# Moving two batches of a decoder's last feed-forward block into the attention loop of later batches, in 32 pieces

## The chip, the core and the metric

One core of one Trainium2 chip runs the whole program. The metric is the device time of one execution in microseconds (us), lower is better. A core has five engines that run their own queues in order: TensorE (PE, with its weight loads PEld), VectorE (DVE), ScalarE (ACT), GpSimd (POOL) and the DMA queue of SyncE (SP).

## What is computed

Two decoder layers over x of 4 batches x 512 rows x 256 columns, all float32. The part that matters here is layer 1, after its self-attention: cross-attention of 16 heads against 1601 context rows, a residual and a layer norm, and then a feed-forward block whose weights are dequantized from int32:

```python
scores = jnp.einsum('bhqd,bhkd->bhqk', Q, K) * SCALE        # layer 1 cross-attention
...
h = (x - mu) * jax.lax.rsqrt(var + EPS) * ln_gamma + ln_beta  # the last block
y = jax.nn.silu(h.reshape(-1, H) @ w1 + fc1_bias)             # 256 -> 1024
z = y @ w2 + fc2_bias                                         # 1024 -> 256
return residual + 0.5 * z.reshape(residual.shape)
...
x = _layernorm(x + _L1_ffn_ref(x, ...))
```

In that last line the block's residual is x itself, so the sum is 2x + 0.5 z. Batches are independent of one another through all of layer 1.

## The kernel before

Layer 1 is one instruction order written out by hand (a manual schedule: each engine runs its instructions as the Python code emits them). Its attention is a loop over `units` (line 1208): for self-attention and then for cross-attention, for each batch b, four groups g of four heads. A cross-attention unit has 13 steps k over the context rows (12 of 128 rows and one of 65), each of two halves of two heads. A half emits, in this order (lines 1848 to 1860): a score matmul (`scores`, line 1467), the two matmuls of a "slot" of the next unit that serve its row maxima (`slot1`, line 1419, recorded as line 202 with tiles one<-kc,qt), the second score matmul, two exponentials on ScalarE (`exponents`, line 1481), two maximum reductions on VectorE (`reduce`, line 1424), and half of the weighted sum of the step before (`weighted`, line 1494, tile po). Scores contract over 32 rows, so the two scores and the two slot matmuls of a half sit in four different row groups of the array and run together; the trace counts every float32 matmul as two records.

Other work is put between these steps by three lists for each unit. `starts` runs ahead of a unit. `extras` are spread evenly over its steps, at the end of a step; in a step that takes one (`filled`, line 1839) the whole weighted sum goes into the first half as one matmul of 512 columns instead of two of 256. `quiet` gives up one item after each half, and what is left at the unit's end runs at once. The last unit has no slots left; it emits all four scores of a step together.

Score tiles come from a pool of three PSUM banks (`spare`, tag s2), slots and most extras from one of four (`one`).

Cross-attention of batch b ends in `finish` (line 1504): copy of po, transposes, division (`divided`), two transposes (`turned`), four projections (`projected`) and a layer norm (`normalize_apart`), all as extras and quiet items of the next batch's first unit. Two units later `block_input(b)` (line 1622) norms again, transposes into xT[b] and makes 2x plus a bias on GpSimd (`twice`). The block's weights f1 and f2 are loaded and multiplied out by eight `dequantized` items in the quiet list of the unit (3, 2), that is batch 3, group 2 (line 1815). They use the tiles raw and swp, which the rotary step `rotated` (line 1294) also uses.

The block itself, `block(b)` (line 1650), runs for all four batches after the last unit. A `first(f)` makes 128 of the 1024 hidden columns for 512 rows: two matmuls of 512 columns into one bank and one Silu on ScalarE. A `second(t)` makes 128 output rows: eight matmuls of 256 columns, and a VectorE instruction that adds to x. After each second row tile come the final layer norm (on VectorE, with the reciprocal root by Newton steps, `rstd_newton`) and the store. The end of batch 3's own cross-attention, its two norms and its `block_input`, the generator `ending`, is dealt out one item after each piece of the block:

```python
firsts, seconds = zip(*(block(b) for b in range(B)))
rest = ending()
for work in (firsts[0], firsts[1], seconds[0], firsts[2], seconds[1], firsts[3], seconds[2], seconds[3]):
    if work is firsts[3]:
        for _ in rest:
            pass
    for f in work:
        f()
        next(rest, None)
```

Of the kernel before, what the change touches and what calls it, by code (L numbers as in the profile page):

```python
# [9 lines left out]
F32 = mybir.dt.float32  # L10
# [29 lines left out]
def decoder(ctx: ExitStack, tc: tile.TileContext, a: dict, out: bass.AP):  # L40
# [587 lines left out]
    with tc.tile_pool(name="p2", bufs=2) as p2, ExitStack() as ordered:  # L628
# [538 lines left out]
    with ExitStack() as s4:  # L1167
# [137 lines left out]
        def flush(n):  # L1305
            while len(going) > n:
                going.pop(0)()
# [342 lines left out]
        def block(b):  # L1650
# [46 lines left out]

            return [lambda f=f: first(f) for f in range(NF)], [lambda t=t: second(t) for t in range(NT)]


        order1 = [(u, s) for u in units for s in range(slots1(u))]
        ends1, n = {}, 0
# [109 lines left out]
        work = [loads[0], loads[1], nothing, nothing]  # L1812
        for i in range(8):
            work += [products[i], loads[i + 2] if i < 6 else nothing, nothing]
        quiet[index[3, 2, True]] += work

        for i, u in enumerate(units):
            for f in starts[i]:
                f()
            nk = NKT if u[2] else NT  # L1820
            work = extras[i]
            ran = 0
            alone.append(u)
            while done["n"] < ends1[u] + LEAD:
                reduces = [next1() for _ in range(min(2, ends1[u] + LEAD - done["n"]))]
                for f in reduces:
                    f()
                if ran < len(work) - nk // 2:
                    work[ran]()
                    ran += 1  # L1830
            alone.clear()
            del work[:ran]
            ran = 0
            for k in range(nk):
                behind = (u, k - 1)
                if k == 0:
                    behind = (units[i - 1], (NKT if units[i - 1][2] else NT) - 1) if i else None

                filled = ran < len(work) and ran * nk < (k + 1) * len(work)
                if u == units[-1]:  # L1840
                    pairs = [[scores(u, k, half, h) for h in range(2)] for half in range(2)]
                    for half in range(2):
                        next1()
                        exponents(u, k, half, pairs[half])
                        if quiet[i]:
                            quiet[i].pop(0)()
                    weighted(*behind)
                for half in range(2 if u != units[-1] else 0):
                    first = scores(u, k, half, 0)
                    reduce = next1()  # L1850
                    exponents(u, k, half, (first, scores(u, k, half, 1)))
                    reduce()
                    if quiet[i]:
                        quiet[i].pop(0)()
                    if behind is None:
                        pass
                    elif not filled:
                        weighted(*behind, half * 256, half * 256 + 256)
                    elif half == 0:
                        weighted(*behind)  # L1860
                while filled and ran < len(work) and ran * nk < (k + 1) * len(work):
                    work[ran]()
                    ran += 1
            while ran < len(work):
                work[ran]()
                ran += 1
            while quiet[i]:
                quiet[i].pop(0)()
        weighted(units[-1], NKT - 1)

        def ending():
# [19 lines left out]

    late_a.close()
    late_w.close()
# [139 lines left out]
```

## Time and profile before

| what | us |
|---|---|
| runs | 2378.8, 2392.78, 2396.34; median 2392.78 |
| the profiled execution | 2391.23, its span 2389.1 |
| cross-attention, 16 units | 1456 to 2265.2 |
| of which units (2,1) to (3,3) | 1934.0 to 2265.3 |
| last block and its end | 2265.2 to 2389.1 |
| mean granted clock of TensorE over the span | 0.971 |

How to read it. A timeline line gives the start in us from the span's start, the time from the start of the first to the end of the last of the records that it merges, the engine, the line of the kernel, the operation, what is written and read, the shapes, how many records, and in brackets how long the engine had been idle and what ended that. A windows line gives, for a stretch of time, its length and then the busy time (and the count) of PE, PEld, DVE, ACT and POOL, the granted TensorE clock, and the DMA share and rate. A line "a/b/c" of one source line gives the shortest, median and longest duration in ns.

### The profile page before, as it was taken

To read this page: it belongs to the slowest core of one execution; us is meant where nothing else is said; L and a number is where in the kernel's file an instruction comes from. 1 tells how busy PE (TensorE), PEld (TensorE's weight loads), DVE (VectorE), ACT (ScalarE), POOL (GpSimd) and SP (SyncE) were. 2 spreads that over 40 slices of the span, in tenths; PEclk is the share of its full clock that TensorE was granted. 3 is DMA by queue.
4 is the path that set the end of the run, shared out by engine and by line. 5 is a ranking of instruction groups with operands and counts; after the bars stand their busy time and mean duration, and the time that the engine had idled before them with its cause. 6 is when DMAs were issued, how large, how long until landed. Compare 5 with 4: busy or idle time off the path is not lost.

```text
span 2389.1 us, 36156 instructions
## 1 busy us (share of the span) xinstructions
PE 2270.9 (95%) x14448; PEld 1287.5 (54%) x14448; DVE 1231.9 (52%) x2918; ACT 1063.0 (44%) x2103; POOL 369.3 (15%) x383
## 2 busy tenths in 40 slices
PE   7899999977999999879999999999999999999998
PEld 4768577756888988633333334333333333333366
DVE  1433334431333434455656667666766776777234
ACT  1111222223554645424555443655656565666730
POOL 1010001130222122335230010211112010000000
PEclk9999999988999999989999998999999999999999
DMA  8400311135887767352221310112110010100000
GB/s 302 177 0 1 133 55 46 46 126 190 333 307 269 291 260 297 108 173 85 67 87 54 116 37 1 38 33 72 63 39 28 25 60 15 64 1 21 29 9 27
DMA packets 77099, 244.13 MB, mean 102 GB/s; under 512 B 11640, under 2 KB 34686, under 8 KB 64638
## 3 DMA queue, kind: packets, MB, share of 16 engines
q1 hardware_dynamic: 60126, 141.96, 17.2%
q0 software_dynamic: 13632, 89.32, 9.9%
q10 hardware_dynamic: 3168, 10.48, 1.2%
q8 instruction: 116, 1.90, 0.3%
q14 instruction: 57, 0.47, 0.1%
HBM read 196.12 MB, written 56.77 MB: 106 GB/s over the span
## 4 chain that ended last, share of the span: by engine, by line
PE 53%; ACT 1%; DVE 1%; DMA 1%; POOL 1%; issue 0%; SPq 0%; DVEq 0%; ACTq 0%; POOLq 0%
PE s L1467 23%; PE one L202 12%; PE po L1494 12%; PE s L202 3%; PE s L1477 1%; PE one L1452 1%; PE one L1515 1%; DMA cx<-in_ctxT 1%; ACT x L171 1%; DVE one L1426 0%; ACT ex L1481 0%; DMA y<-ys,yrows 0%; DVE pm L1424 0%; PE one L1536 0%; DMA qd<-q 0%
## 5 line engine op out<-in xcount | busy, mean ns | idle before, releaser
L1481 ACT ACTIVATE ex<-s 128x512 f32<-128x512 f32 (+1 forms) x1062 | 578.0, 594 | 465.5 <-PE s L1467 225.3
L1424 DVE TENSOR_REDUCE pm<-one 128x1 f32<-128x512 f32 x768 | 492.8, 685 | 161.1 <-PE s L1467 106.1
L1467 PE MATMUL s<-q,kc 32*128 32x512 f32 x1612 | 528.8, 639 | 0.8 <-ACT ex L1481 0.8
L202 PE MATMUL one<-kc,qt 32*128 32x512 f32 (+1 forms) x2048 | 483.5, 563 | 0.3 <-DVE pm L1424 0.3
L1467 PEld LDWEIGHTS s<-q,kc 32*128 32x128 f32 x1612 | 166.1, 179 | 203.1 <-issue 170.0
L1494 PE MATMUL po<-ex,v 128*32 128x256 f32 (+3 forms) x2688 | 251.5, 443 | 0.3 <-ACT ot L1507 0.3
L1426 DVE CUSTOM_DVE_ANT_0 one<-one,c_diagq 128x512 f32<-128x512 f32 x256 | 171.9, 715 | 97.8 <-PE one L202 88.2
L1494 PEld LDWEIGHTS po<-ex,v 128*32 128x32 f32 (+1 forms) x2688 | 54.1, 108 | 253.1 <-issue 246.4
L1467 PE MATMUL s<-q,ks 32*128 32x512 f32 x512 | 180.6, 658 | 6.2 <-ACT ex L1481 4.9
L202 PEld LDWEIGHTS one<-kc,qt 32*128 32x128 f32 x2048 | 164.5, 188 | 11.8 <-DVE pm L1424 7.4
L202 PE MATMUL bank<-eWo,g 128*128 128x256 f32 x608 | 140.3, 387 | 11.5 <-DVE rb L997 8.2
L202 PE MATMUL one<-ks,qt 32*128 32x512 f32 x512 | 149.6, 664 | 0.0
L202 PE MATMUL wide<-xbT,eWi 128*128 128x128 f32 (+1 forms) x960 | 141.0, 308 | 4.0 <-DVE xbT L943 4.0
L977 DVE TENSOR_TENSOR g<-g,sg 128x1024 f32<-128x1024 f32 x38 | 46.4, 1224 | 180.3 <-ACT sg L975 171.9
L202 PEld LDWEIGHTS wide<-xbT,eWi 128*128 128x128 f32 x960 | 131.1, 194 | 13.4 <-issue 4.2
L202 PE MATMUL wide<-xbT,eWg 128*128 128x128 f32 (+1 forms) x960 | 137.0, 303 | 0.0
L202 PEld LDWEIGHTS bank<-eWo,g 128*128 128x128 f32 x608 | 115.5, 194 | 31.0 <-DVE rb L997 12.2
L1299 POOL TENSOR_TENSOR raw<-raw,c_cos 128x512 f32<-128x512 f32 (+1 forms) x32 | 35.0, 1093 | 626.5 <-DVE swp L1298 626.5
L202 PEld LDWEIGHTS wide<-xbT,eWg 128*128 128x128 f32 x960 | 128.1, 191 | 6.6
L1467 PEld LDWEIGHTS s<-q,ks 32*128 32x128 f32 x512 | 53.4, 187 | 83.9 <-issue 64.6
L975 ACT ACTIVATE g<-wide,eWi 128x128 f32<-128x128 f32 (+1 forms) x240 | 72.6, 410 | 56.8 <-PE wide L202 56.4
L202 PE MATMUL wide<-ctxT,q 128*128 128x512 f32 (+1 forms) x256 | 91.3, 510 | 0.8 <-DVE q L669 0.8
(346 smaller groups left out, 2948.5 us busy)
## 6 DMA issues: line engine op xcount, KB each, us to landing
xs<-zero SPq DMA_DIRECT2D x32, 512.0 KB
kc<-kcd SPq DMA_DIRECT2D x16, 800.5 KB
eWo<-in_eWo SPq DMA_DIRECT2D x8, 1408.0 KB
eWi<-in_eWi SPq DMA_DIRECT2D x8, 1028.0 KB
eWg<-in_eWg SPq DMA_DIRECT2D x8, 1028.0 KB
qt<-qd SPq DMA_DIRECT2D x32, 256.0 KB
ctxT<-in_ctxT SPq DMA_DIRECT2D x4, 1601.0 KB
cx<-in_ctxT SPq DMA_DIRECT2D x12, 512.0 KB
```

The costliest lines, as they stand in the source:

```text
L171: nc.scalar.activation(into(t), xb[:, t, :], AF.Identity, scale=mid["rs"][:, t : t + 1], bias=mid["nb"][:, t : t + 1],)
L202: nc.tensor.matmul(ps, l, r, start=(i == 0), stop=(i == n - 1))
L975: nc.scalar.activation(dst[:, k, :], pv[:, k, :], func, bias=bias)
L977: nc.vector.tensor_tensor(part, part, dst, ALU.mult)
L1299: eng.tensor_tensor(raw[:, :n], raw[:, :n], cos[:, :n], ALU.mult)
L1424: nc.vector.tensor_reduce(pm[:, t, j, c : c + 1], ps, AX.X, ALU.max)
L1426: nc.vector.tensor_tensor_reduce(out=ps, in0=ps, in1=diagq[:, 384 - t * P : 896 - t * P], scale=1.0, scalar=LOWEST, op0=ALU.add, op1=ALU.m ...
L1452: nc.tensor.transpose(pt[:, t * P : (t + 1) * P], ng.rearrange("p j r -> p (j r)"), ident)
L1467: nc.tensor.matmul(ps[:kn], kt[rows, k * P : k * P + kn], q2[rows, :], start=True, stop=cross)
L1477: nc.tensor.matmul(ps[:, k * P : (k + 1) * P], later_[:, :P], later_[:, P:], start=False, stop=True)
L1481: nc.scalar.activation(ex[:kn, h, :], ps[:kn], AF.Exp)
L1494: nc.tensor.matmul(state["po"][j * 32 : j * 32 + 32, q0:q1], (vals if cross else vself)[b % 2][:kn, k, c0 : c0 + 32], ex[:kn, j % 2, q0:q1 ...
```

## The change

The last block of batches 0 and 1 leaves the end of the program and runs as `extras` of later cross-attention units: 16 pieces for batch 0 in units (2,1), (2,2), (2,3), 16 for batch 1 in (3,0) to (3,3). A new function makes the pieces. Silu is replaced by h times exp(-(ln(1 + exp(-m)) + m - h)) with m = max(h, -40), which is made of exponential and logarithm alone. A list of callbacks (`pending`) delays the ScalarE instructions: `logarithm` runs two halves after its piece, `gate` two halves after that; `settle` runs them at once where something depends on them.

```diff
         def rotated(raw, n, ks, eng, tables=None):
             cos, sin = tables or (cosT[:, ks], sinT[:, ks])
+            settle()
...
+        pending = []
+        def tick():
+            for p in pending:
+                p[1] += 1
+            while pending and pending[0][1] >= 2:
+                pending.pop(0)[2]()
+        def settle(upto=None):
+            while pending and (upto is None or pending[0][0] <= upto):
+                pending.pop(0)[2]()
...
+        def block_apart(b):
+            held = {}
+            def first(q, f0):
+                flush(0)
+                settle(count[0] - 2)
...
+                if f0 == 0:
+                    held[q] = p4.tile([P, 2, 512], F32, tag="cx", name="cx", bufs=2)
+                h = held[q][:, f0 // 4, :]
+                ps = one()
+                for i in range(4):
+                    w = f1[f0 // 4], f1[2 + f0 // 4]
+                    mm(
+                        ps[:, i * P : (i + 1) * P],
+                        [(w[c][:, i * P : (i + 1) * P], xT[b][:, c, q * P : (q + 1) * P]) for c in range(2)],
+                    )
+                nc.vector.tensor_tensor(
...
+                    ALU.add,
+                )
+                m = raw_tile()
+                nc.gpsimd.tensor_scalar(m, h, -40.0, None, ALU.max)
+                e = p4.tile([P, S + 1], F32, tag="swp", name="swp")[:, :S]
...
+                def logarithm():
+                    nc.scalar.activation(e, m, AF.Exp, scale=-1.0)
+                    nc.scalar.activation(e, e, AF.Ln, bias=state["unit"])
+                    nc.gpsimd.tensor_tensor(m, m, h, ALU.subtract)
+                    nc.gpsimd.tensor_tensor(e, e, m, ALU.add)
+                    pending.append([me, 0, gate])
+                def gate():
+                    nc.scalar.activation(e, e, AF.Exp, scale=-1.0)
+                    nc.gpsimd.tensor_tensor(h, h, e, ALU.mult)
+                pending.append([me, 0, logarithm])
...
+            def second(q, c):
+                settle(held[q, "last"])
+                ps = one()[:, :P]
...
+                        (
+                            held[q][:, f // 4, (f % 4) * P : (f % 4 + 1) * P],
+                            f2[f // 2][:, (f % 2) * D + c * P : (f % 2) * D + (c + 1) * P],
+                        )
+                        for f in range(NF)
...
+                nc.vector.scalar_tensor_tensor(
+                    out=at, in0=ps, scalar=0.5, in1=at, op0=ALU.mult, op1=ALU.add
+                )
+                if c == 1 and q == NT - 1:
+                    _, pairs, ends = normalize_apart(x[b], rstd=rstd_newton)
+                    store = lambda: nc.sync.dma_start(out[b].rearrange("(t p) d -> p t d", p=P), x[b])
+                    for i, f in enumerate(pairs + ends + [store]):
+                        pending.append([held[q, "last"], -i, f])
+            order = "F0 F0 F1 F1 S0 S0 F2 F2 S1 S1 F3 F3 S2 S2 S3 S3".split()
...
-        quiet[index[3, 2, True]] += work
+        quiet[index[2, 0, True]] += work
+        for b, first_unit, n in ((0, index[2, 1, True], 3), (1, index[3, 0, True], 4)):
+            pieces = block_apart(b)
+            for k in range(n):
+                share = -(-len(pieces) // (n - k))
+                extras[first_unit + k] += pieces[:share]
+                pieces = pieces[share:]
...
-        firsts, seconds = zip(*(block(b) for b in range(B)))
+        (firsts2, seconds2), (firsts3, seconds3) = block(2), block(3)
         rest = ending()
-        for work in (firsts[0], firsts[1], seconds[0], firsts[2], seconds[1], firsts[3], seconds[2], seconds[3]):
-            if work is firsts[3]:
+        for work, n in ((firsts2, 1), (seconds2, 2), (firsts3, 0), (seconds3, 0)):
+            if work is firsts3:
                 for _ in rest:
                     pass
             for f in work:
                 f()
-                next(rest, None)
+                for _ in range(n):
+                    next(rest, None)
```

`tick()` is called after every half's quiet item. A piece F (`first` above) makes half of the 1024 hidden columns for one tile of 128 rows; a piece S (`second`) makes 128 of the 256 output columns for that tile.

More of the change, by code (lines that the diff above doesn't have):

```diff
@@ L1698, in block @@
             return [lambda f=f: first(f) for f in range(NF)], [lambda t=t: second(t) for t in range(NT)]
+        pending = []
[7 more added lines that the diff above has]
+                pending.pop(0)[2]()
+        count = [0]
+        def block_apart(b):
[3 more added lines that the diff above has]
+                settle(count[0] - 2)
+                me = count[0]
+                count[0] += 1
+                if f0 == 0:
[9 more added lines that the diff above has]
+                nc.vector.tensor_tensor(
+                    h.rearrange("p (k n) -> p k n", n=P),
+                    ps.rearrange("p (k n) -> p k n", n=P),
+                    b1f[:, f0 : f0 + 4, None].to_broadcast([P, 4, P]),
+                    ALU.add,
[3 more added lines that the diff above has]
+                e = p4.tile([P, S + 1], F32, tag="swp", name="swp")[:, :S]
+                if "unit" not in state:
+                    state["unit"] = p4c.tile([P, 1], F32, tag="unit", name="unit")
+                    nc.gpsimd.memset(state["unit"], 1.0)
+                def logarithm():
[8 more added lines that the diff above has]
+                pending.append([me, 0, logarithm])
+                held[q, "last"] = me
+            def second(q, c):
+                settle(held[q, "last"])
+                ps = one()[:, :P]
+                mm(
+                    ps,
+                    [
+                        (
[3 more added lines that the diff above has]
+                        for f in range(NF)
+                    ],
+                )
+                at = x[b][:, q, c * P : (c + 1) * P]
+                nc.vector.scalar_tensor_tensor(
+                    out=at, in0=ps, scalar=0.5, in1=at, op0=ALU.mult, op1=ALU.add
+                )
+                if c == 1 and q == NT - 1:
[4 more added lines that the diff above has]
+            order = "F0 F0 F1 F1 S0 S0 F2 F2 S1 S1 F3 F3 S2 S2 S3 S3".split()
+            pieces, seen = [], {}
+            for o in order:
+                q, n = int(o[1]), seen.get(o, 0)
+                seen[o] = n + 1
+                pieces.append((lambda q=q, n=n: first(q, 4 * n)) if o[0] == "F" else (lambda q=q, n=n: second(q, n)))
+            return pieces
@@ L1846, in decoder @@
                             quiet[i].pop(0)()
+                        tick()
                     weighted(*behind)
@@ L1854, in decoder @@
                         quiet[i].pop(0)()
+                    tick()
                     if behind is None:
@@ L1868, in decoder @@
                 quiet[i].pop(0)()
+        settle()
         weighted(units[-1], NKT - 1)
```

## Prediction

> **What bounds the kernel now.** I read the page's first part, then stretches by unit, the timeline of single steps, and the last 124 us. Stretches of two ordinary units and of the last two stages (columns: stretch, length, busy PE, PEld, DVE, ACT, POOL, granted clock, DMA share, GB/s):
>
> ```profile
> PE 2270.9 (95%) x14448; PEld 1287.5 (54%) x14448; DVE 1231.9 (52%) x2918; ACT 1063.0 (44%) x2103; POOL 369.3 (15%) x383
> ...
> 2139.46:2188.37 48.91, 48.91 (x428) 16.66 (x432) 33.27 (x62) 30.16 (x57) 5.12 (x2) 0.97 0.00 1
> 2188.37:2237.12 48.75, 48.75 (x400) 16.22 (x400) 33.41 (x58) 30.85 (x58) 0.00 (x0) 1.00 0.20 61
> 2237.12:2265.28 28.16, 27.84 (x201) 7.07 (x197) 0.68 (x2) 25.28 (x50) 0.00 (x0) 1.00 0.00 1
> 2265.28:2389.10 123.82, 116.00 (x420) 77.76 (x420) 45.48 (x208) 30.15 (x46) 5.13 (x2) 0.98 0.05 18
> ```
>
> PE is busy throughout, both where the pieces go and where they come from. So the move pays only if a piece costs the loop less than its share of the end. What a step costs is read from the starts of its score matmuls: an unfilled step, a step with an extra of one projection, and the ScalarE lines of the former:
>
> ```profile
> 2051.23 0.69 PE L1467 MATMUL s<-q,kc 32*128 32x512 f32 x1
> ...
> 2053.08 0.69 PE L1467 MATMUL s<-q,kc 32*128 32x512 f32 x1
> ...
> 2054.72 0.69 PE L1467 MATMUL s<-q,kc 32*128 32x512 f32 x1
> ```
> ```profile
> 1896.92 0.69 PE L1467 MATMUL s<-q,kc 32*128 32x512 f32 x1
> ...
> 1900.27 1.13 PE L202 MATMUL one<-xaO,atT 128*128 128x256 f32 x4
> 1901.33 0.69 PE L1467 MATMUL s<-q,kc 32*128 32x512 f32 x1
> ```
> ```profile
> 2052.39 1.09 ACT L1481 ACTIVATE ex<-s 128x512 f32<-128x512 f32 x2 [0.49 <-PE one L202]
> 2054.30 1.08 ACT L1481 ACTIVATE ex<-s 128x512 f32<-128x512 f32 x2 [0.82 <-PE s L1467]
> ```
>
> Unfilled: 2054.72 - 2051.23 = 3.49. Filled: 1901.33 - 1896.92 = 4.41 here, its neighbours 4.26 (their starts are 1904.76, 1909.02 and so on); I use 4.26. So the projection, 4 records of 256 columns at 0.214 = 0.86 on PE, costs 4.26 - 3.49 = 0.77: all but 0.09 of itself. There is hardly a hole to fill. ScalarE has one, 0.49 or 0.82 a half; VectorE (33 of 49 us) has room too.
>
> **The change, part by part.**
>
> Removed from the end: two `firsts` and two `seconds`. The chain of waits and the timeline have them:
>
> ```profile
> 2312.37 13.73 PE one L202 x32
> 2326.11 13.81 PE s L202 x64
> ```
>
> 2 x (13.73 + 13.81) = 55.1 us. PE is without a gap there, so all of it leaves the path.
>
> Added to the loop: 32 pieces. Each is 8 products of 128 columns, 16 records; 512 in all, in place of 64 of 512 and 128 of 256 columns. The row for 128-column records with their own weight loads is in the expert layer, at full clock:
>
> ```profile
> 703.79 7.31 PE L202 MATMUL wide<-xbT,eWi 128*128 128x128 f32 x64
> ```
>
> 7.31 / 64 = 0.114, against 0.107 by columns alone (13.73 / 32 / 4). [...] The row has the same full-array shape and shows the load hidden, so I take 0.114: a piece is 1.83, and 32 x (1.83 - 0.09) = 55.7 us. The last unit has no slots and its ScalarE is the fuller engine (25.28 of 28.16), but PE is at 27.84; its four S pieces use no ScalarE and I give them the same price.
>
> ScalarE: each of the 16 F pieces brings Exp and Ln in a row (2 x 0.59 = 1.2, the duration of the exponentials) and later one Exp (0.59). In the stretch that is 28 us on an engine idle for over a third, and no table switch: `rstd_ln` already runs Ln and Exp between exponentials. But three score banks leave no reserve: the next half's second score waits for this half's first exponential, as the 1.85 against 1.64 of the two halves shows. 1.2 meets a gap of 0.49 or 0.82 (mean 0.65), so 0.55 is left; about half of the time the next piece follows in that step and PE's 1.74 covers it. 16 x 0.28 = 4.5 us. The single Exp fits its gap. Bounds: 0, and all 1.8 uncovered, 29 us. I stay near the low end because the two delays are long enough: m needs about 0.2 + 0.69 (VectorE, the row of line 1456) + 1.4 (GpSimd, half of the 2.77 of `twice`) = 2.3 us after the piece, and Exp comes over 4 us after it (one half and the next one's scores and exponentials); the gate needs two GpSimd instructions of 1.27 (rotary rows) = 2.5 after Exp, and comes two halves, 3.5, later. If that cover were gone, the next exponentials stand behind the waiting one, then the score banks, then PE.
>
> VectorE: 0.69 per F and some 0.3 per S beside 1.74 more of PE; nothing. GpSimd: 5.2 us per F, one F in 5 us or more; nothing. If GpSimd fell behind, S pieces would wait on PE, which an order with two other pieces between F and its S prevents.
>
> Weights: the 16 loads and 8 products move from unit (3,2) to (2,0), 26 halves for 28 items. On SP they now stand before batch 3's keys and values, which are first needed some 140 us later; nothing. The norm of batch 1 stays at that unit's end as before. `settle` in the rotary step of (2,3) can make ScalarE wait for GpSimd once, under 2 us; a Newton root of batch 0 (12 small instructions, 2.6 us on VectorE) falls into the loop, 1 to 2 us. Against it, in (3,0) the first piece pushes batch 2's norm off the unit's end, where it now costs about 2 us. Together +1.
>
> The end: batch 3's chain. Before, it ran under three `firsts` and a `seconds`:
>
> ```profile
> 2297.09 0.14 PEld L1634 LDWEIGHTS one<-ident,ln 128*128 128x128 f32 x1 [0.24 <-issue]
> 2297.52 0.60 PE L1634 MATMUL one<-ident,ln 128*128 128x128 f32 x4
> ```
>
> Now only block 2 covers it: from the end of the last unit, `firsts2` with transposes and projections takes 18.6 us (2265.2 to 2283.8 today), `seconds2` 13.7, so PE is out of work at 32.3. Meanwhile VectorE does in order: root (to 20.5), sum of tile 0 (22.7), shift; ScalarE applies (25.1); sum and norm of the first tile pair, 4.4 (to 30.3: 2305.50 to 2309.9 today); statistics 1.8 (32.1); sum 0.4; second root 2.6 and shift (35.3); ScalarE applies four times 0.54 (37.6); transposes and copies (39.2). PE idles 5.3 us, and with the short transposes about 5.9 us are lost. Then the clock:
>
> ```profile
> 1025.00:1036.40 11.40, 0.21 (x1) 0.00 (x0) 0.00 (x0) 0.37 (x1) 5.88 (x7) 0.70 0.77 247
> 1036.40:1040.00 3.60, 3.49 (x12) 2.19 (x12) 0.00 (x0) 0.37 (x1) 0.00 (x0) 0.52 1.15 481
> ```
>
> After an idle PE of 11 us, work runs at 0.52. [...] I take 1.7. The end shrinks by 55.1 - 5.9 - 1.7 = 47.5 us.
>
> Sum: -47.5 + 55.7 + 4.5 + 1 = +13.7. The profiled execution took 2391.2, so 2404.9, say **2405 us**; the median of the runs, 2392.8, is 1.6 above it, so +12 to +14, 0.5%.
>
> **Rivals.**
> (1) Slower: ScalarE's added instructions stall the loop. For it: three banks, no reserve, in-order queues through GpSimd and back. Against: gaps of 0.49 to 0.82 and two halves of delay. It decides from about 1.0 us per F piece: 16.4 instead of 4.5 gives 2417, over 1% above the median; at 1.3 to 1.8 it is 2421 to 2429.
> (2) Faster: the pieces fill holes that PE's busy time hides. For it: the 1.85 half is 0.21 longer than the other, and unit (3,2), with two transposing extras more than (3,1), is no longer (48.75, 48.91). Against: the projection paid 0.77 of 0.86, and (3,1) lost time at a clock below 1. It ends below the median if a piece costs at most about 1.3; at 1.2, with ScalarE hidden: 2391.2 - 47.5 + 38.4 + 1 = 2383. Over 1% faster needs 0.8 a piece, less than half of its own PE time.
> (3) The chain of batch 3 is longer or the clock stays low for 10 us: another 5 to 8 us, 2412.
> That the pieces don't stand where the text puts them is excluded by the instruction order of the built kernel.
>
> **How the numbers follow.** Likeliest 0.60 (own range 2395 to 2416), rival 1 0.18, rival 2 0.12, rival 3 0.10. Range 2388 to 2424: rival 2's lower half and the top of rival 1 are left out. 1% (24 us, about what can be told from no change) puts the bounds at 2369 and 2417: slower 0.18 x 0.75 + 0.60 x 0.05 + 0.10 x 0.3 = 0.20; faster 0.02; same 0.78.
>
> **What would show it.** Steps with a piece at 5.2 us against 3.49 (4.7 for rival 2; long idle before exponentials released by GpSimd for rival 1). Cross-attention ends near 2327. From there to the end about 76 us, with one idle PE of 5 to 6 us ahead of the transposes of batch 3 and a granted clock near 0.5 after it. The forecast is wrong if 128-column records in the loop don't run at 0.114, or if ScalarE waits for GpSimd.

## The result, and the profile after

| what | before | after |
|---|---|---|
| median of 15 runs each, us | 2387.78 | 2398.05 |
| ratio, 95% interval | | 1.0046, 1.0034 to 1.0059 |
| span of the profiled execution, us | 2389.1 | 2393.0 |

The change makes the kernel slower by 0.46%, 10 us, which is within the 1% that the forecast called "same": 2405 was forecast, 2398 came.

The two spans differ by only 3.9 us, and that isn't the size of the change. Everything ahead of unit (2,0) is the same program in both, yet (2,0) starts at 1881.9 us in the one trace and at 1876.5 in the other; among all the traces of this study the start lies anywhere from 1867 to 1887. From there on a program repeats itself closely: units that an edit doesn't touch agree to 0.02 us. So I measure from that start, with the copies of po (the weighted sums of the preceding unit) on ScalarE as the units' bounds (us). A copy stands in the first step of a unit: in the first half if that step is filled, otherwise one half, 1.6 us, later. So (3,0), which begins with a piece after the change and not before, starts 1.6 us earlier there: what counts to (2,3) before counts to (3,0) after. The sums over the units are not touched by this.

| unit | before | after |
|---|---|---|
| (2,0), takes the weights | 52.12 | 53.71 |
| (2,1), 6 pieces | 51.68 | 63.25 |
| (2,2), 5 pieces | 48.97 | 58.13 |
| (2,3), 5 pieces | 51.10 | 57.95 |
| (3,0), 4 pieces | 53.69 | 61.37 |
| (3,1), 4 pieces | 48.92 | 55.33 |
| (3,2), 4 pieces; before: the weights | 48.75 | 57.00 |
| (3,3), 4 pieces | 28.16 | 34.85 |
| the eight units | 383.39 | 441.59 |
| from there to the end | 123.80 | 74.95 |
| from (2,0) to the end | 507.19 | 516.54 |

The loop grows by 58.2, the end shrinks by 48.85, and 9.35 us are lost. The page of the changed kernel, part 1:

```profile
PE 2272.1 (95%) x14536; PEld 1300.3 (54%) x14536; DVE 1240.4 (52%) x2912; ACT 1084.1 (45%) x2143; POOL 454.9 (19%) x448
```

PE is as busy as it was, in a span that is longer: nothing that stood idle has been filled. The stretches of units (2,1), (3,2) and (3,3) and of the end after the change (columns as before: stretch, length, busy PE, PEld, DVE, ACT, POOL, granted clock, DMA share, GB/s):

```profile
1930.20:1993.45 63.25, 63.25 (x482) 27.56 (x484) 38.39 (x73) 38.87 (x73) 24.93 (x20) 0.97 0.10 35
...
2226.23:2283.23 57.00, 57.00 (x444) 24.28 (x448) 31.15 (x55) 34.30 (x63) 10.00 (x9) 1.00 0.01 1
2283.23:2318.09 34.86, 34.86 (x254) 13.21 (x255) 5.51 (x27) 27.14 (x55) 5.77 (x3) 1.00 0.00 1
2318.09:2393.00 74.91, 62.74 (x227) 41.54 (x225) 30.81 (x128) 19.40 (x31) 5.14 (x2) 0.95 0.06 22
```

In the units with pieces PE has no gap at all, and ScalarE (38.9 of 63.3, 34.3 of 57.0) is far from full. In the end PE stands still for 12 us of 75 (before 8 of 124), and its clock is lower.

Single steps, as the timeline has them: an unfilled step begins at 2020.61, a step with a `second` at 2024.04, the one behind it at 2029.34:

```profile
2020.61 0.69 PE L1468 MATMUL s<-q,kc 32*128 32x512 f32 x1
...
2024.04 0.69 PE L1468 MATMUL s<-q,kc 32*128 32x512 f32 x1
...
2027.35 2.05 PE L202 MATMUL one<-f,cx 128*128 128x128 f32 x16
2029.34 0.69 PE L1468 MATMUL s<-q,kc 32*128 32x512 f32 x1
```

Unfilled 3.43, filled 5.30; ahead of the last unit a filled step takes 5.12 to 5.39 in most cases. A piece costs some 1.8 us of loop. From its first record to the start of the score matmul behind it it holds PE for 1.98 to 1.99 (2027.35 to 2029.34).

The end, with VectorE's last root, ScalarE's four applications, and the transposes of batch 3:

```profile
2351.84 0.16 DVE L166 SCALAR_TENSOR_TENSOR nb<-mv,rstd 128x4 f32<-128x4 f32 x1
...
2352.10 2.07 ACT L171 ACTIVATE ln<-x,nb,rstd 128x256 f32<-128x256 f32 x4 [9.90 <-DVE nb L166]
...
2352.75 0.33 PE L1635 MATMUL one<-ident,ln 128*128 128x128 f32 x1 [2.90 <-ACT ln L171]
...
2353.24 0.33 PE L1635 MATMUL one<-ident,ln 128*128 128x128 f32 x1 [0.16 <-ACT ln L171]
...
2355.42 2.07 PE L202 MATMUL one<-xT,f 128*128 128x512 f32 x2 [0.41 <-ACT xT L1638]
```

PE waits 2.90 us ahead of the transposes and a little before each (the brackets), and the two records of 512 columns at 2355.42 take 2.07 us, where two such records take 1.13 at full clock (trace of before, 2265.18).

There is one more wait, at the end of unit (2,0), which no step of the forecast has. After and then before, the same place:

```profile
1924.29 1.08 ACT L1482 ACTIVATE ex<-s 65x512 f32<-65x512 f32 x2 [0.96 <-PE one L202]
...
1926.51 0.30 ACT L125 ACTIVATE sd<-mv,eps 128x4 f32<-128x4 f32 x1 [1.13 <-DVE mv L161]
...
1927.27 2.07 ACT L171 ACTIVATE x<-x,nb,rstd 128x256 f32<-128x256 f32 x4 [0.23 <-DVE nb L166]
...
1929.25 1.05 ACT L1482 ACTIVATE ex<-s 128x512 f32<-128x512 f32 x2
...
1929.88 1.12 PE L1468 MATMUL s<-q,kc 32*128 32x512 f32 x2 [1.75 <-ACT ex L1482]
...
1930.93 3.17 PE L202 MATMUL one<-xT,xaQ 128*128 128x512 f32 x4
```
```profile
1929.67 0.30 ACT L125 ACTIVATE sd<-mv,eps 128x4 f32<-128x4 f32 x1 [0.93 <-DVE mv L161]
1930.00 0.20 ACT L127 ACTIVATE rstd<-sd 128x4 f32<-128x4 f32 x1
1930.11 1.06 ACT L1481 ACTIVATE ex<-s 65x512 f32<-65x512 f32 x2
...
1931.09 2.08 ACT L171 ACTIVATE x<-x,nb,rstd 128x256 f32<-128x256 f32 x4
...
1933.07 1.05 ACT L1481 ACTIVATE ex<-s 128x512 f32<-128x512 f32 x2
```

Batch 1's norm has three items, the root (sd, rstd) and two with two applications each, and they are put behind what is still in the quiet list. Before, a pair of exponentials stands between the root and the applications: from one pair to the next (1930.11 to 1933.07) it is 2.96 us, and PE has no gap. After, the list has 28 items for 26 halves, so the root too is left over, and all three items run at once at the unit's end, one behind the other: ScalarE waits 1.13 for VectorE's mean and a little for the shift, applies for 2.07, and only then come the exponentials, 4.96 us after the last ones. The score banks are full by then and PE waits 1.75. Then the clock drops, and four records of 512 columns take 3.17; such four take 1.98 at full clock elsewhere in the trace of before.

### The profile page after: what moved, and what is told of

It is laid out like the page before. It is cut to its first block, busy times and chain, and to the rows that moved or that the text cites. A ratio compares the mean times of both kernels' runs of the same rounds, so it can differ in the third digit from the quotient of the medians.

```text
span 2393.0 us, 36441 instructions
## 1 busy us (share of the span) xinstructions
PE 2272.1 (95%) x14536; PEld 1300.3 (54%) x14536; DVE 1240.4 (52%) x2912; ACT 1084.1 (45%) x2143; POOL 454.9 (19%) x448
## 4 chain that ended last, share of the span: by engine, by line
PE 54%; DMA 1%; DVE 1%; ACT 1%; SPq 0%; issue 0%; POOL 0%; DVEq 0%; ACTq 0%
PE s L1468 24%; PE one L202 14%; PE po L1495 12%; PE s L202 1%; PE s L1478 1%; PE one L1453 1%; PE one L1516 1%; DMA kcd<-in_c_rowkc 1%; ACT x L171 1%; DMA cx<-in_ctxT 0%; DVE one L1427 0%; PE one L1537 0%; DMA qd<-q 0%; DMA qd<-raw 0%; ACT ex L1482 0%
## 5 line engine op out<-in xcount | busy, mean ns | idle before, releaser
L1482 ACT ACTIVATE ex<-s 128x512 f32<-128x512 f32 (+1 forms) x1062 | 578.1, 594 | 491.6 <-PE s L1468 252.5
L1495 PE MATMUL po<-ex,v 128*32 128x256 f32 (+2 forms) x2456 | 244.5, 467 | 0.0
```

Source lines behind the costliest of these rows:

```text
L1482: nc.scalar.activation(ex[:kn, h, :], ps[:kn], AF.Exp)
L1495: nc.tensor.matmul(state["po"][j * 32 : j * 32 + 32, q0:q1], (vals if cross else vself)[b % 2][:kn, k, c0 : c0 + 32], ex[:kn, j % 2, q0:q1 ...
```

## The experiments

My theory after the result: the pieces cost what their own PE time says; ScalarE's added work costs next to nothing because the two delays hold; two waits of PE, one at the end of (2,0) and one in batch 3's chain, cost the rest, each by its own length and by a lower clock after it. The rival from the forecast, ScalarE as the cause, stands against it. In the table: the time from unit (2,0) to the end in the profiled execution, and the ratio of the timed runs to the kernel before.

| kernel | (2,0) to end, us | ratio | 95% interval |
|---|---|---|---|
| before | 507.19 | 1 | |
| after | 516.54 | 1.0046 | 1.0034 to 1.0059 |
| e1_no_gate | 514.78 | 1.0041 | 1.0027 to 1.0055 |
| e2_hide_chain | 511.27 | 1.0038 | 1.0024 to 1.0052 |
| e3_norm_spread | 513.58 | 1.0024 | 1.0011 to 1.0037 |
| e4_no_delay | 589.21 | 1.0326 | 1.0306 to 1.0346 |
| e5_batch0_only | 514.47 | 1.0012 | 1.0000 to 1.0023 |
| e6_narrow | 544.99 | 1.0136 | 1.0103 to 1.0169 |
| e7_more_exp | 537.47 | 1.0133 | 1.0109 to 1.0156 |
| e8_both | 509.67 | 1.0009 | 0.9994 to 1.0025 |
| e9_before_early | 504.65 | 0.9979 | 0.9964 to 0.9993 |
| e10_all | 509.83 | 0.9997 | 0.9985 to 1.0009 |
| e11_one_exp | 523.24 | 1.0066 | 1.0048 to 1.0083 |

The ratios carry the noise of the 1870 us ahead of (2,0), some 3 us; where they and the first column differ by that much, only the first column resolves the effect, and it comes from one execution.

For e9_before_early and e10_all the first column has another start: their empty extras make the first step of (2,0) filled, so that the copy which marks the start comes 1.6 us earlier. The first score matmul of (2,0) on PE and the copy, in the kernel before and in e9_before_early:

```profile
1877.91 0.69 PE L1467 MATMUL s<-q,kc 32*128 32x512 f32 x1
...
1881.90 0.59 ACT L1507 COPY ot<-po 128x512 f32<-128x512 f32 x1
```
```profile
1871.93 0.69 PE L1467 MATMUL s<-q,kc 32*128 32x512 f32 x1
...
1874.32 0.59 ACT L1507 COPY ot<-po 128x512 f32<-128x512 f32 x1
```

Between the two lie 3.99 us in the one and 2.39 in the other. For these two kernels I therefore count from the first score matmul: 511.2 us to the end before, 507.0 in e9_before_early, 512.2 in e10_all (its first score at 1865.07), 513.7 in e8_both. In this count the units from (0,1) to (1,3) agree to 0.03 us in all kernels whose edits leave them alone.

### ScalarE's added work: e1_no_gate, e4_no_delay, e7_more_exp, e11_one_exp

e1_no_gate takes the gate out of every `first`:

```diff
-                m = raw_tile()
-                nc.gpsimd.tensor_scalar(m, h, -40.0, None, ALU.max)
...
-                    nc.scalar.activation(e, m, AF.Exp, scale=-1.0)
-                    nc.scalar.activation(e, e, AF.Ln, bias=state["unit"])
...
-                    nc.scalar.activation(e, e, AF.Exp, scale=-1.0)
-                    nc.gpsimd.tensor_tensor(h, h, e, ALU.mult)
```

> Leaves out Exp, Ln, Exp and the four GpSimd instructions of each of the 16 F pieces (the hidden values go on without their gate); all matmuls and VectorE instructions stay. If TensorE alone sets the loop's pace and the added ScalarE work lies in its gaps, only 0 to 4 us go, so 2394 to 2398. If the added ScalarE and GpSimd instructions are what made the kernel slower (rival 1), 8 us or more go and the time is at or below that of the kernel before, 2388 to 2390. If the pieces fill hidden holes in TensorE's time, nothing changes.

Measured: 514.78, so 1.8 us less than the changed kernel, with 16 rows of Exp, Ln and Exp (0.63 + 0.72 + 0.63 each, 32 us of ScalarE) and all their GpSimd work gone. The eight units shrink from 441.59 to 440.52; by chance the lower clock lasts 6.8 us here instead of 3.4 at the end of (2,0), which hides up to 1.7 more. So the gates cost 1.1 to 2.8 us. The first rival, 16 us and more, is out.

e4_no_delay takes away the delays (the items of the two final norms in the loop, which go through the same list, come two halves earlier as well):

```diff
-            while pending and pending[0][1] >= 2:
+            while pending and pending[0][1] >= 0:
```

> The delay of two halves before a piece's logarithm and two before its gate becomes none: both run after the next half, one right behind the other. ScalarE then waits in place for GpSimd's two instructions (2.5 us after the Exp, of which the Ln covers 0.7), and the exponentials stand behind it. If the delay is what keeps ScalarE's work hidden, each of 16 pieces costs about 2 us more: 2420 to 2440. If ScalarE has reserve enough to absorb a wait of 2 us, under 5 us more.

Measured: +72.7 us over the changed kernel, 4.5 a piece, more than expected. ScalarE and PE around one `first` of this kernel in the timeline:

```profile
1963.55 0.63 ACT L1750 ACTIVATE swp<-raw 128x512 f32<-128x512 f32 x1 [0.53 <-POOL raw L1743]
1964.21 0.72 ACT L1751 ACTIVATE swp<-swp,unit 128x512 f32<-128x512 f32 x1
1966.90 0.63 ACT L1757 ACTIVATE swp<-swp 128x512 f32<-128x512 f32 x1 [1.97 <-POOL swp L1753]
1967.43 1.55 ACT L1482 ACTIVATE ex<-s 128x512 f32<-128x512 f32 x3
...
1968.07 1.12 PE L1468 MATMUL s<-q,kc 32*128 32x512 f32 x2 [2.41 <-ACT ex L1482]
1969.12 1.92 PE L1495 MATMUL po<-ex,v 128*32 128x512 f32 x8
```

ScalarE waits for GpSimd twice (0.53, 1.97), the exponentials (L1482) stand behind it, and PE has no bank for 2.41 us. Then the weighted sum takes 1.92 where 1.06 is usual: the clock is down. Summed over this trace, PE's waits of over 0.6 us between (2,0) and the end of the loop come to 31 us (1.75 in the changed kernel), and the spells at half clock there to 75 us (3.4), which cost up to half their length: 29 + 36 = 65 of the 73. About half of the price is the clock behind the waits, not the waits.

e7_more_exp and e11_one_exp put two more, or one more, Exp of the same values in the row of each `first` (the lines of e7_more_exp; e11_one_exp has `range(2)`):

```diff
-                    nc.scalar.activation(e, m, AF.Exp, scale=-1.0)
+                    for _ in range(3):
+                        nc.scalar.activation(e, m, AF.Exp, scale=-1.0)
```

> Each F piece makes its first Exp three times instead of once (two that repeat the same result), 1.26 us more of ScalarE in a row, 20 us in all. If ScalarE's gaps and the matmuls of the next piece take most of it, 2 to 8 us more than the changed kernel: 2400 to 2406. If ScalarE sets the pace there, all 20: 2418.

> The changed kernel with one Exp more in each of the 16 pieces of the first layer (the same values once again, in a row with the other Exp and the Ln): the row on ScalarE is 2.0 us instead of 1.39. Two more gave +20.9 us, 1.3 a piece, as much as their own time. If the changed kernel stands just at the edge of what the gap and the three score banks cover, one more costs its whole 0.65 too: 16 x 0.65 = +10 us over the changed kernel. If there is a reserve of some half us, one more costs 0 to 4 us and the second one carries the rest.

Measured: two more cost 20.9 us over the changed kernel, as the rival had it and not I; one more costs 6.7, between the two cases that I had set. The timeline of e7_more_exp:

```profile
1970.80 1.95 ACT L1751 ACTIVATE swp<-raw 128x512 f32<-128x512 f32 x3 [0.63 <-POOL raw L1743]
1972.79 0.72 ACT L1752 ACTIVATE swp<-swp,unit 128x512 f32<-128x512 f32 x1
1973.41 1.55 ACT L1482 ACTIVATE ex<-s 128x512 f32<-128x512 f32 x3
...
1974.04 1.12 PE L1468 MATMUL s<-q,kc 32*128 32x512 f32 x2 [1.33 <-ACT ex L1482]
```

Against it, the same place in the changed kernel:

```profile
2023.41 1.09 ACT L1482 ACTIVATE ex<-s 128x512 f32<-128x512 f32 x2 [0.56 <-PE one L202]
2024.38 0.63 ACT L1750 ACTIVATE swp<-raw 128x512 f32<-128x512 f32 x1
2025.05 0.73 ACT L1751 ACTIVATE swp<-swp,unit 128x512 f32<-128x512 f32 x1
2025.67 1.06 ACT L1482 ACTIVATE ex<-s 128x512 f32<-128x512 f32 x2
2027.26 1.09 ACT L1482 ACTIVATE ex<-s 128x512 f32<-128x512 f32 x2 [0.53 <-PE one L202]
```

In the changed kernel the exponentials follow the Ln with no gap, and the pair after them has an idle 0.53 before it again: the row's 1.29 us (2024.38 to 2025.67) fit. One more Exp is 0.65 us and costs 6.7 / 16 = 0.42, so the reserve left is about 0.2 us a piece. The second costs (20.9 - 6.7) / 16 = 0.89, of which some 0.3 is half clock (13.6 us of such spells before the end, against 3.4). So the forecast's "next to nothing" holds by a margin of 0.2 us, on an engine that is idle for a third of the time. The page's busy shares would have told neither number.

### The width of the products: e6_narrow

Each product of a `first` is made in two halves of 64 columns, with the weights loaded for each:

```diff
+                    for z in range(0, P, 64):
+                        mm(
+                            ps[:, i * P + z : i * P + z + 64],
...
+                                (w[c][:, i * P : (i + 1) * P], xT[b][:, c, q * P + z : q * P + z + 64])
```

> Each product of the F pieces is made in two halves of 64 columns with the same weights loaded twice: the same multiplications in 512 records more, 32 for each F piece instead of 16. If a weight load of 128 columns takes about 0.107 us and hides under 128 columns but not under 64, a record still takes 0.107 to 0.114 and each F piece 1.7 us more: 16 x 1.7 = 27 us, 2425. If the load were never a limit, no change, 2398. [...]

Measured: +28.5 us for 256 records more (16 pieces with 16 more each; the 512 of the expectation are all that they then have). The half clock lasts 6.8 us instead of 3.4 at two places, which hides up to 1.7 each: 25 to 27 us, 1.6 to 1.7 a piece. One piece of it in the timeline, loads and matmuls (in the changed kernel such a piece has x16 and 2.05):

```profile
2021.80 3.65 PEld L202 LDWEIGHTS one<-xT,f 128*128 128x128 f32 x32 [0.76 <-issue]
2021.80 3.79 PE L202 MATMUL one<-xT,f 128*128 128x64 f32 x32
```

(3.79 - 2.05) / 16 = 0.109 for each added record, though the columns are the same in sum. In the trace the records of a piece start 0.112 us apart with 128 columns and with 64, where by columns alone it would be 0.107 and 0.054 (13.73 / 32 / 4 and half of it). The expectation's 0.107 us for a load is shown by no run; what the traces show is the loads' pace: 0.108 to 0.112 us from one to the next in the changed kernel's piece at 2027.35 (each load's record is 0.19 long, and the records overlap), and with 32 of them in 3.65 us (3.65 less the last one's 0.19, over 31) 0.112 here. So I read it thus, as an estimate from these numbers: the loads go at their own pace beside the matmuls; with 128 columns a record that pace is about the matmuls' own and the loads are hidden, with 64 it sets the time. Every record here has its own load, so another fixed cost of such a record would look the same; it is not the issuing, for records in different row groups start 0.007 us apart (four of them from 2020.61 on in the changed kernel). That loads and matmuls of one piece don't take turns shows in the changed kernel's piece at 2027.35: its 16 loads span 1.86 us and its 16 matmuls 2.05, both from 2027.35 on.

### The chain of batch 3 and the norm of batch 1: e2_hide_chain, e3_norm_spread, e8_both

e2_hide_chain lets batch 3's chain go first: its items are dealt out ahead of each `second` of batch 2, and the two final norms of batch 2 follow only before batch 3's `seconds`:

```diff
+                if b == 2:
+                    late_norms.append(lambda: norm_pair(t))
+                else:
+                    norm_pair(t)
...
+            if work is seconds3:
+                for f in late_norms:
+                    f()
             for f in work:
+                if work is seconds2:
+                    for _ in range(n):
+                        next(rest, None)
                 f()
...
```

> Only the end is changed: the final norm of batch 2 is emitted after the first products of batch 3, and the steps of batch 3's chain stand ahead of batch 2's second products instead of behind them. If the exposed chain costs its idle TensorE (2.9 us, and some 0.9 between the transposes) and the half clock after it (1.7), the time falls by about 5 us to 2393, the trace shows no idle TensorE of over 1 us there and no clock of 0.5 before the end. If that gap is hidden by something else, no change.

Measured: 511.27, 5.3 less than the changed kernel. 4.1 are the end (70.86 instead of 74.95), 1.2 a spell of half clock in unit (2,1) that did not come in this execution. The transposes in its timeline:

```profile
2347.26 2.07 ACT L171 ACTIVATE ln<-x,nb,rstd 128x256 f32<-128x256 f32 x4 [6.16 <-DVE nb L166]
...
2347.92 0.33 PE L1635 MATMUL one<-ident,ln 128*128 128x128 f32 x1 [0.62 <-ACT ln L171]
```

PE's wait has gone from 2.90 to 0.62, and no lower clock follows. So 4.1 of the chain's 6.25 us (55.1 less 48.85) are shown: 2.3 of waiting, and 1.7 or so of clock. Of the 2.1 that remain, the 0.62 and three waits of 0.16 between the transposes are 1.1; the rest I haven't traced.

e3_norm_spread drops eight of the empty items among the weights in the quiet list of unit (2,0), so that the list is empty in time and the norm's root comes with a half of its own again:

```diff
-            work += [products[i], loads[i + 2] if i < 6 else nothing, nothing]
+            work += [products[i], loads[i + 2]] if i < 6 else [products[i], nothing]
```

> The eight empty items of the dequantizing list in unit (2,0) are left out but two, so that batch 1's norm is dealt out one item a half, as in the kernel before, and is not run at once at the unit's end. If that burst (1.75 us of idle TensorE, then a half clock for 3.4 us) is one of the costs, 2 to 3 us go: 2395 to 2396. If not, 2398.

Measured: 513.58, 3.0 less. Unit (2,0) is back to 52.13 (before 52.12), the wait of 1.75 is gone, and unit (2,1) takes 62.06 instead of 63.25, as the half clock doesn't come. The four applications still run in a row at the unit's end, as before the change; it was the root beside them that made PE wait. The weights are still loaded in this unit, so it was not they.

> The reordered end of e2 and the shortened list of e3 together. Their savings are at different places (about 4 us at the end, 1.6 at the end of unit (2,0) and 1.2 of half clock after it) and should add: 7 us from the start of unit (2,0), about 2391, 2 to 3 us above the kernel before. If they overlap, 2394.

e8_both has both edits: 509.67, 6.9 less than the changed kernel, the sum of 4.1 and 2.8. What remains over the kernel before is 2.5 us.

### Half of the move: e5_batch0_only

Batch 0 alone goes into the loop; batch 1's block stays at the end:

```diff
-        for b, first_unit, n in ((0, index[2, 1, True], 3), (1, index[3, 0, True], 4)):
+        for b, first_unit, n in ((0, index[2, 1, True], 3),):
...
-        (firsts2, seconds2), (firsts3, seconds3) = block(2), block(3)
+        (firsts1, seconds1), (firsts2, seconds2), (firsts3, seconds3) = block(1), block(2), block(3)
...
```

> Only batch 0 moves; batch 1's block goes back to the end, between batch 2 and batch 3. Counted from the start of unit (2,0): the units of batch 2 grow as in the changed kernel (29 us), the end shrinks by one block (27.5) and no longer by less, since batch 3's chain has two blocks to hide under. If TensorE's own time is all that moves, this lies 1 to 3 us above the kernel before (2390), well under the changed kernel. If each moved batch costs the same net loss (about 5 us), 2393.

Measured: +7.3 over the kernel before from (2,0) on (the ratio, +0.12%, would be +3; the trace is one execution). Too high for my expectation by 4 to 6. The end is 27.5 shorter, one whole block (13.73 + 13.81 = 27.54), so with batch 1's block as cover the chain costs nothing. The loop grows by 34.8. I take it apart by the units' first score matmuls, which don't move with the copies. The three units with pieces, (2,1) to (2,3), grow by 28.0 in e3_norm_spread: the 16 pieces alone, 1.75 each. Here they grow by 32.3; the 4.3 on top are the burst at (2,0) and its clock, twice as long in this execution. (3,0) grows by 2.4. Batch 0's final norm falls there, with its Newton root on VectorE:

```profile
2112.26 0.37 DVE L161 BATCH_NORM_AGGREGATE mv<-st 128x2 f32<-128x6 f32 x4
...
2114.85 0.16 DVE L142 SCALAR_TENSOR_TENSOR rstd<-part,rstd 128x4 f32<-128x4 f32 x1
2114.93 1.28 DVE L1425 TENSOR_REDUCE pm<-one 128x1 f32<-128x512 f32 x2
...
2115.68 0.66 PE L1516 MATMUL one<-ident,ot 128*128 128x128 f32 x4 [0.99 <-DVE pm L1425]
```

The maximum reduction, which frees a bank, stands behind the root, and PE waits 0.99 for it; I take the rest of the 2.4 for the same norm's, but haven't followed it to single instructions. I had left the burst, which the changed kernel's trace already showed, and this norm out of the expectation.

### Is anything gained by the move? e9_before_early, e10_all

If the place of a norm is worth so much, the kernel before may profit too. e9_before_early adds four empty extras to the first units of batches 1, 2 and 3; extras are spread evenly, so the projections and the norm of the preceding batch come earlier:

```diff
+        for b in (1, 2, 3):
+            extras[index[b, 0, True]] += [nothing] * 4
```

> The kernel before, with four empty extras added to the first unit of batches 1, 2 and 3. They do no work, but the extras are spread evenly over a unit, so the projections and the norm of the preceding batch now come earlier and the norm no longer meets the unit's end. My theory: part of what the change costs is not the pieces but where the preceding batch's norm falls (a burst at the unit's end, 1.6 to 2 us each); then the kernel before profits as well, by 2.5 to 4 us from unit (2,0) to the end: 503 to 505 against 507.2, a ratio of 0.998 to 0.999. The rival: the burst costs only where the pieces and weights lie (the emptied quiet list of unit (2,0)), and before there is nothing to gain: 507, ratio 1.000.

Measured, from the first score of (2,0): 507.0, 4.1 less than before, at the far end of what was expected, and 0.9979 (0.9964 to 0.9993) in the timed runs. (The 504.65 of the table seem to say 2.5, because the count starts 1.6 us earlier.) 1.2 of it lie where (2,0) meets (2,1) and 2.95 where (3,0) meets (3,1); of these, 1.7 are a spell of half clock that had come in (3,1), behind the burst, and is gone. It is the fastest kernel here, and it has none of the change in it.

e10_all puts such empty extras, for batches 1 and 2, into e8_both:

> The changed kernel with both repairs (norms of batch 2 delayed past the chain of batch 3, the norm of batch 1 clear of the end of unit (2,0)) and with the empty extras in the first units of batches 1 and 2. From unit (2,0) to the end the two repairs gave 509.7; unit (2,0) has its norm spread already, so I expect 509 to 510 here and a gain only before it, in unit (1,0), 1 to 2 us: ratio to the kernel before 1.000 to 1.001. It should not beat the kernel before with the same empty extras: the pieces' own 0.114 for 128 columns and their ScalarE work stay.

Measured: 0.9997 (0.9985 to 1.0009), as fast as the kernel before, no faster. From the first score of (2,0) it takes 512.2: 1.0 more than before, 1.4 less than e8_both, and 5.2 more than e9_before_early. The gain ahead of (2,0) that I expected is missing: units (1,0) and (1,1) together take 0.2 us less, not 1 to 2, in this kernel and in e9_before_early. The two have neither a wait of PE over 0.4 us nor a spell of half clock in the loop, so they show the move itself. Loop: 438.96 - 380.85 = +58.1. End: 70.87 - 123.8 = -52.9.

## Why the prediction was right, and where it was off

| term | forecast | measured | from |
|---|---|---|---|
| two blocks leave the end | -55.1 | two times -27.5 | e5: one block, -27.5 |
| chain of batch 3: idle PE | +5.9 | about +4.5 | 55.1 - 48.85 = 6.25, less 1.7 of clock; e2 shows 2.3 of it |
| clock after it | +1.7 | +1.7 | 3.4 us at 0.51 |
| 32 pieces on PE, with `settle` and batch 0's root | +55.7 and +3 | +55.6 to +57.3 | the remainder, see below |
| ScalarE's gates | +4.5 | +1.1 to +2.8 | e1 |
| batch 2's norm off the end of (3,0) | -2 | about -3, of which 1.7 clock | e9 against before |
| batch 1's norm at the end of (2,0) | 0 | +2.8 | e3: 1.6 and 1.2 |
| sum | +13.7 | +9.35 | |

**The pieces.** 58.2 is the loop's whole growth; less 2.8 for the burst, less 1.1 to 2.8 for the gates, and plus the 3.0 that the kernel before lost at the end of (3,0), it leaves 55.6 to 57.3, 1.74 to 1.79 for a piece against 1.74. Since this term is a remainder, the table's sum comes out by itself; but e10_all against e9_before_early gives nearly the same without the burst and without the spell, 58.1 less the gates, 55.3 to 57.0. So the central step held: the work costs the loop nearly all of its PE time. That the 1.74 fits so closely is luck in part. The records of a piece do start 0.112 us apart, as those of the expert layer do, but some 0.2 us lie between the first and the second and again behind the last, so a piece holds PE for 1.98 and not 1.83; and a step takes up 0.2 of it and not 0.09. The two errors cancel. The row of the expert layer, with its loads hidden at 0.114 a record, decided rightly: from 703.80 to 711.10 its loads and its matmuls are both busy for all of the 7.30 us, in the changed kernel's pieces they run side by side as well, and e6_narrow fits it. Batch 0's root was put at 1 to 2 us. In e5_batch0_only, where (3,0) has no pieces, that unit is 2.4 longer; in the changed kernel it is 1.1 to 1.3 longer than four pieces at 1.76 make it.

**ScalarE.** The estimate took half of the rows as uncovered by 0.55. The trace shows the row fitting nearly everywhere: its waits for GpSimd are 0.7 us in all. The mechanism, a row in a gap with little reserve, was right and e4, e7 and e11 show it at work; the size was 2 to 3 us too high.

**The chain.** The forecast had an idle PE of 5 to 6 us, and 2.90 came, because the step added four applications (2.2 us) ahead of the first transpose. The transposes go tile by tile: the first follows the first application (2352.10 and 2352.75 in the lines above). The root and its shift ended 34.7 us after the last weighted sum (forecast 35.3) and PE ran out of work after 32.6 (32.3). No run of the kernel before shows the forecast's 1.7 us for the lower clock: there the spell around the idle PE of 11 us lasts 10.24 (1029.64 to 1039.88, at 0.50). What the changed kernel showed in its place is 0.51 for 3.4 us, which loses 1.7.

**Batch 1's norm.** "The norm of batch 1 stays at that unit's end as before" was costed at nothing. The applications stayed; the root joined them, and together they cost 1.75 of waiting and then clock. The forecast even has the reason, 28 items in 26 halves, and draws nothing from it. This step failed; e3 shows its price, 2.8. The opposite term, batch 2's norm pushed off the end of (3,0), was counted with 2: e9 finds 3.0 there, of which 1.7 are the clock that followed in that execution. It also finds 1.2 at the end of (2,0), a sign that even before the change the applications there were not free, though the trace shows no wait of PE.

**What the profile was to show.** Filled steps at 5.2: 5.30 above, most 5.12 to 5.43. Cross-attention ending near 2327: it ends at 2318.1, of which 5.4 is the earlier start of (2,0) and the rest the 3 us by which the loop grew less. The end at 76: 75. One idle PE before the transposes and half clock: yes, of half the length.

The errors partly cancelled: 2.8 too little at (2,0), some 7 too much in the other terms. Over all kernels the answer stands: neither place is better. On PE a piece takes 1.98 in the loop in eight narrow products, and 55.1 / 32 = 1.72 in wide ones at the end; the loop gives back 0.2 to 0.25 of it, and the end has lost cover for its chain.

What stays open: some 1 us of the chain's price, and how the remainder in the table divides between the pieces, `settle` and the root.

## What to carry to other kernels

Work moved from a stage where an engine is full to another where the same engine is full brought nothing here (10 us lost, with ScalarE idle for a third of the time): read from a neighbouring step what share of an added matmul a step absorbs (here a tenth), and compare the price of the same work in the two shapes. Before adding instructions to an in-order engine inside a tight loop, measure its gap in one half-step and the number of buffers that stand between it and the next engine; here the average idle share was a third, and the reserve 0.2 us. When a list of work gets longer, look at what stands behind it: two items too many pushed a root onto four applications, for 2.8 us. And when stages are compared across kernels, take a mark that the edits don't move: here the copies of po hid 1.6 us of a gain of 4.1.

## What the hardware did that I had not expected

The clock fell to half after far shorter waits than the 11 us that the forecast had gone by. Three stretches of the changed kernel (the first is what follows the wait at the end of (2,0), the others the wait in the chain and what follows it):

```profile
1931.60:1935.00 3.40, 3.40 (x8) 0.92 (x10) 0.00 (x0) 0.94 (x2) 0.00 (x0) 0.50 0.17 70
2349.85:2352.75 2.90, 0.00 (x1) 0.00 (x0) 2.54 (x14) 0.65 (x2) 0.00 (x0) 1.00 0.00 0
2354.80:2358.20 3.40, 2.99 (x6) 1.23 (x5) 3.19 (x8) 1.24 (x2) 3.32 (x2) 0.51 0.00 0
```

A wait of 1.75 us at 1928.1 was followed by 3.4 us at 0.50 that began 3.5 us after the wait's start; a wait of 2.90 at 2349.9 likewise, 5.0 us after its start. The spells in all traces last 3.4 us or a multiple (6.8, 10.2), and each 3.4 costs up to 1.7. They followed waits as short as 0.8 and 0.9 us in e7_more_exp, 0.2 in the kernel before (at 2139, the spell that e9_before_early is without), and did not always come: e2_hide_chain has the same 1.75 at (2,0) and no spell.

The traces show what this mostly hangs on. Within each of them all spells begin on one grid of 3.413 us, to 0.005: in e4_no_delay at 1938.46, 1969.18, 1982.84 and 2037.45, which is 9, 4 and 16 such intervals apart, and in the changed kernel at 1931.58 and 2354.84, 124 apart. How a wait lies on the grid decides in most cases. The intervals around the same 1.75, first in the changed kernel, then in e2_hide_chain:

```profile
1928.17:1931.58 3.41, 1.71 (x4) 0.71 (x5) 2.77 (x7) 3.41 (x8) 0.00 (x0) 1.00 0.98 420
```
```profile
1927.44:1930.86 3.42, 2.76 (x22) 0.46 (x14) 2.82 (x11) 2.02 (x7) 0.00 (x0) 1.00 0.99 370
1930.86:1934.27 3.41, 2.32 (x5) 0.97 (x6) 2.15 (x5) 2.98 (x7) 0.00 (x0) 1.00 0.98 420
```

In the one PE is idle for half of one interval (by the matmuls' ends as the trace models them), and the next runs at half clock; in the other the wait is split over two, 0.19 and 0.32 of them idle, and none does. From (2,0) to 15 us before the end of PE's work, over all 13 traces, 19 of 21 intervals with 0.45 or more idle are followed by one at half clock, 8 of 25 with 0.2 to 0.45 begin a spell, and 3 of some 1900 with less. So no sharp bound shows, and the spell in the kernel before at 2139 is one of the three exceptions. In these traces a stall of PE of 1 to 3 us cost between once and nearly twice its length, by where it fell: the end of (2,0) cost 1.6 and then 1.2 of clock in the changed kernel and had no spell behind it in e2_hide_chain; in e4_no_delay the clock took 36 us and the waits 29.
